# A fixed order for a program's beginning: transfers by need, the first group's norms on VectorE, its queries batch by batch

## The chip, the core and the metric

The kernel runs on one core of a Trainium2 chip. The metric is the device time of one launch in microseconds (us). Four executions of the kernel before took 1539.61 to 1543.85 us, with a median of 1542.02 us.

The names of the engines are those of the profile: PE (TensorE, matrix products; PEld is its loading of weights), DVE (VectorE), ACT (ScalarE), POOL (GpSimd) and SP (SyncE, which here issues nearly all transfers, in the order of its queue). Each engine runs its own instructions strictly in order and waits, by semaphores, for results of the others.

## The reference

Two transformer layers over x (64 batches of 128 rows of 128 numbers). Layer 0 attends from the normed x to 128 rows of a side input and 120 rows of a context, with 16 heads of 8, and then sends each row to two of eight experts. Layer 1 attends to the context alone and has small experts of its own. Everything is float32. Cut to its frame:

```python
x = x + _L0_xattn_ref(_layernorm(x), fside_BxSxS_0, ctx_1024, ctx_1024, ...)
x = x + _L0_ffn_ref(_layernorm(x), L0_ffn_wqkv, L0_ffn_w1, L0_ffn_w2)
x = x + _L1_xattn_ref(_layernorm(x), ctx_1024, ctx_1024, ...)
x = x + _L1_ffn_ref(_layernorm(x), L1_ffn_Wg, L1_ffn_bg, L1_ffn_W1, L1_ffn_W2)

def _L0_xattn_ref(x1, x2, memory_k, memory_v, Wq, bq, Wk, bk, Wv, bv, Wp, bp):
    q = heads(x1 @ Wq + bq)
    k = heads(concatenate([x2 @ Wk + bk, memory_k], axis=1))
    v = heads(concatenate([x2 @ Wv + bv, memory_v], axis=1))
    attn = softmax(einsum('bhqd,bhkd->bhqk', q, k) * scale)
    return merge(einsum('bhqk,bhkd->bhqd', attn, v)) @ Wp + bp
```

## The kernel before

The 64 batches stand in 16 groups of 4 (`GB`), and x stays in SBUF, one tile of [128, 4, 128] per group (`xg`). The attention of layer 0 is one loop over iterations `it`, a software pipeline: iteration `it` computes the row maxima of batch `it` (`max_bank`: products L344 on PE, reductions L356 on DVE), adds them as a shift to the queries of the batch before (`shift`: transposes L401, DVE L404), computes the shifted scores of batch `it - 2` and their exponentials (`score_bank`: L372 on PE, L380 on ACT), multiplies the exponentials of batch `it - 3` with the values (`values`: L417), and finishes batches `it - 3` and `it - 4` (`out1` to `out5`). The rounds of an iteration come in two halves, `rounds(0, 1)` and `rounds(2, 3)`, of four banks for the maxima and four for the scores each. All products go through eight PSUM banks that are handed out in turn (`mtile`).

Queries, keys and values of a group are made in the iterations ahead of it (`prep`): in a regular group, keys (`prep_k`: L187 on PE, L192 on ACT) and values (`prep_v`: L199 on PE, L206 on DVE) when `it` is 2 modulo 4, the transposed normed rows (`prep_x`: L165 on PE, L166 on ACT) when it is 3, and the queries (`prep_q`: L269 on PE, four activations L273 on ACT, one for each of four slots) when it is 0, two activations in each half.

The norms of layer 0 are split: DVE takes statistics of each batch (`Norm.stats`, L113), and POOL puts them together for a group of four in nine small operations (`put_together`, L127 to L135, of which the last is a power), makes the normed rows (`normed`, L156) and then adds the output bias to x (L465).

The beginning lies outside the hand-ordered part of the program (`tc.manual_schedule`, within which the engines keep the order in which the code names their instructions); there the scheduler places instructions by its own priorities. SP's queue begins with four groups of x, the three masks, eight tensors of layer 0's weights and biases, a block of zeros for the experts' rows, the router's weights and three constants, and then kvT of group 0 (the side input, transposed), the context's keys and values (`context`, L247 and L250), and kvT of group 1; twelve more groups of x and layer 1's weights follow. Before the loop, all of group 0 is prepared, for four batches at a time: keys, values, transposes, queries. Group 1's transposes and queries (`norm_of(1)`, `prep_x(1)` and `prep_q(1, ·)`) are placed in iterations 0 and 1.

Layer 1 begins in another way: `prep_batch(j)` (L284 to L301) makes the queries of one batch of group 0, with one transpose (L293), one copy (L294), one product (L296) and four activations of 128 columns (L298), batch 0 ahead of the loop and the others in the first three iterations. In layer 0 this function isn't used before the change.

The lines of the kernel that the text speaks of are these; an instruction's line in the profile is the line here.

Of the kernel before, what the change touches and what calls it, by code (L numbers as in the profile page):

```python
# [8 lines left out]
F32 = mybir.dt.float32  # L9
# [9 lines left out]
GB = 4  # L19
NG = B // GB  # L20
S = 128
# [23 lines left out]
def transformer_kernel(ctx, tc, a, out):  # L45
# [29 lines left out]
    def load_row(name, n):  # L75
        return load_const(name, [128, n], a[name].partition_broadcast(128))

    def attention_weights(p):
        return dict(
            wq=load_const(p + "wq", [D, D], a[p + "wq"]),  # L80
            wk=load_const(p + "wk", [D, D], a[p + "wk"]),
            wv=load_const(p + "wv", [D, D], a[p + "wv"]),
            wo=load_const(p + "wo", [D, D], a[p + "wo"]),
            bq=load_const(p + "bq", [128, NS], a[p + "bq"]),
            bk=load_const(p + "bk", [128, NV], a[p + "bk"]),
            bv=load_row(p + "bv", D),
            bo=load_row(p + "bo", D),
        )

    hmask = load_const("hmask", [128, NS], a["hmask"])  # L90
    kmask = load_const("kmask", [128, NV], a["kmask"])
    smask = load_const("smask", [128, NV], a["smask"])
    l0 = attention_weights("a0_")


    stat = ctx.enter_context(tc.tile_pool(name="stat", bufs=4))
# [2 lines left out]
    class Norm:  # L99
# [18 lines left out]

        def put_together(self, g):

# [26 lines left out]
                self.mv[:, b0:b1, 0], self.mv[:, b0:b1, 0], -1.0, 1.0, ALU.mult, ALU.mult  # L147
            )

        def normed(self, g, pool=rows, bufs=1, width=D, xn=None, js=range(GB)):  # L150

            if xn is None:
                xn = pool.tile([S, GB, width], F32, name="xn", tag="xn", bufs=bufs)
            for j in js:
                b = g * GB + j
                nc.gpsimd.tensor_scalar(  # L156
                    xn[:, j, :D], xg[g][:, j, :], self.mv[:, b, 0:1], self.rstd[:, b : b + 1],
                    ALU.add, ALU.mult,
                )
            return xn  # L160
# [13 lines left out]
    for s in range(2):  # L174
        k = keep.tile([128, NV, GB, KF + KC], F32, name=f"k2_{s}", tag=f"k2_{s}")
        K2.append(k)
        v = keep.tile([KF, GB, H // 2, 2, 32], F32, name=f"v_{s}", tag=f"v_{s}")
        nc.gpsimd.memset(v, 0.0)
        for i in range(2):
            nc.gpsimd.memset(v[:, :, :, i, 16 * i + HD : 16 * i + HD + 1], 1.0)  # L180
        VS.append([v])
        m = keep.tile([S, 2, 128], F32, name=f"nm_{s}", tag=f"nm_{s}")
        nc.gpsimd.memset(m, 0.0)
        NM.append(m)

    def keys_of(w, src, g, n0, pk):
        nc.tensor.matmul(  # L187
# [29 lines left out]
    def attention(layer, w, norm, first, aside):  # L217
# [5 lines left out]
        with ExitStack() as es:  # L223
# [13 lines left out]
            def loads(g):  # L237
# [2 lines left out]
                nc.sync.dma_start(t, a["fsideT" if first else "ctxT"][:, g * GB : (g + 1) * GB, :])  # L240
                src[g] = t

            def context(g):
                if first:
                    s = g % 2
                    for v in range(NV):
                        nc.sync.dma_start(  # L247
                            k2[s][:, v, :, KF:], a["ctx_k"][:, v, g * GB : (g + 1) * GB, :]
                        )
                    nc.sync.dma_start(  # L250
                        vs[s][1].rearrange("k b h i w -> k b (h i w)"),
                        a["ctx_v"][:, g * GB : (g + 1) * GB, :],
                    )

            def mtile():
                return banks.tile([128, 512], F32, name="bank", tag="bank")
# [204 lines left out]
            def norm_of(g):  # L461
                if g < NG:
                    normed[g] = norm.normed(g)

                    nc.gpsimd.tensor_tensor(  # L465
                        xg[g], xg[g], w["bo"].unsqueeze(1).to_broadcast([S, GB, D]), ALU.add
                    )

            if first:
                loads(0)  # L470
                context(0)
                yield
                norm_of(0)
                prep_k(0)
                prep_v(0)
                prep_x(0)
                prep_q(0, 0)
                prep_q(0, 1)
            else:
                prep_batch(0)  # L480
            loads(1)
            oTs, pos_ = {}, {}

            for it in range(B + (4 if first else 5)):
# [24 lines left out]
                if first:  # L509

                    on(3, out2)
                    prep(it, 0)
                    rounds(2, 3)
                    on(1, shift)
                    on(3, out3)
                    aside.call(it, mtile)
                    on(4, out4, out5)
                    aside.ahead(it)
                    prep(it, 1)
                    aside.call(it, mtile)  # L520
                    aside.end(it, work, mtile)
                else:
                    if it < GB - 1:
                        prep_batch(it + 1)
                    prep(it, 0)
                    on(4, out3)
                    on(3, out2)
                    on(5, out4)
                    prep(it, 1)
                    on(1, shift)  # L530
                    on(5, out5)
                    aside.ahead(it)
                    if it == GB - 1 or it > GB and it % GB == 1:
                        norm_of(it // GB + 1)
                    if it == 1:

                        nc.gpsimd.tensor_tensor(
                            xg[0], xg[0], w["bo"].unsqueeze(1).to_broadcast([S, GB, D]), ALU.add
                        )
# [171 lines left out]
    def logits1(rt, lg, n, l):  # L711
# [16 lines left out]
    nc.vector.memset(zero, 0.0)  # L728
    filled = []


    spare = nc.sync.dma_start(
        xs[E * CAP - TT :].rearrange("(h p) d -> p h d", p=S),
        zero,
    )
    AFTER = mybir.DependencyInfo(mybir.DependencyClass.Sync, mybir.DependencyReason.DATA)
    DEEP = 4
    scatters = []

    def behind(ins, earlier):  # L740
        for e in earlier:
# [2 lines left out]
    def scatter(probe, j, k, xn):  # L744
# [11 lines left out]
        behind(s, [scatters[-DEEP] if len(scatters) >= DEEP else spare])  # L756
        tc.add_to_no_dep_group("scatters", s.ins)
        scatters.append(s)

# [314 lines left out]
    class Aside0(Ahead):  # L1074
# [8 lines left out]
        def lead(self, b):  # L1083
            norms[0].stats(b)
            if b % GB == GB - 1:
                norms[0].roots(b + 1 - GB, b + 1)

        def made(self, b):
            norms[1].stats(b)

# [12 lines left out]
            for _ in self.tiles:  # L1103
                pass

    wr0 = load_const("wqkvT", [D, 3 * E], a["wqkvT"])
# [3 lines left out]
    rp = ctx.enter_context(tc.tile_pool(name="route", bufs=1))  # L1110
    aside0 = Aside0()
    steps = attention(0, l0, norms[0], True, aside0)
    next(steps)
    for b in range(GB):
        aside0.lead(b)
    next(steps)
    for g in range(4, NG):
        load_x(g)
    l1 = attention_weights("a1_")
# [248 lines left out]
```

## Time and profile before

| | us |
|---|---|
| median of 4 runs (lowest, highest) | 1542.02 (1539.61, 1543.85) |
| the profiled execution | 1541.85 |
| its span, first to last instruction | 1540.1 |
| PE busy in the span | 1423.1 (92%) |
| DVE busy | 1057.0 (69%) |
| ACT busy | 838.4 (54%) |
| POOL busy | 641.6 (42%) |

A row of a timeline has the start, the length, the engine, the line, the operation, what it writes and reads, the shapes, and a count if several stand together; in brackets is the idle time of the engine ahead of it and what ended it. PE's float32 products appear as two passes each, so a group of 16 products is a row of x32. The chain of waits is followed back from the last instruction; each of its rows is what the end depended on at that moment.

SP's own rows show how the beginning's transfers are issued (start, time taken by the issue):

```profile
0.74 2.09 SPq L58 DMA_DIRECT2D x<-in_x  x4
...
11.07 0.43 SPq L240 DMA_DIRECT2D kvT<-in_fsideT  x1
11.55 0.98 SPq L247 DMA_DIRECT2D k<-in_ctx_k  x2
12.57 0.56 SPq L250 DMA_DIRECT2D vc<-in_ctx_v  x1
13.18 0.36 SPq L240 DMA_DIRECT2D kvT<-in_fsideT  x1
13.59 16.26 SPq L58 DMA_DIRECT2D x<-in_x  x12
```

### The profile page before, as it was taken

How to read it: one execution, taken by the hardware profiler on the slowest of the kernel's cores; microseconds unless marked ns; L12 is line 12 of the kernel's file. 1: busy time of each engine (PE TensorE's matmuls, PEld its weight loads, DVE VectorE, ACT ScalarE, POOL GpSimd, SP SyncE). 2: the span in 40 equal slices, each digit the busy share in tenths (PEclk: the TensorE clock that was granted, in tenths of full speed). 3: DMA queues.
4: the chain of work that ended last, by engine and by line, in shares of the span. 5: the costliest groups of instructions: out<-in, count | busy, mean ns of one | idle time of the engine just before them, and what ended most of it. 6: DMA issues, size and time to landing. Idle time of an engine off the chain costs nothing.

```text
span 1540.1 us, 44916 instructions
## 1 busy us (share of the span) xinstructions
PE 1423.1 (92%) x18156; PEld 1149.2 (75%) x18156; DVE 1057.0 (69%) x2923; ACT 838.4 (54%) x1722; POOL 641.6 (42%) x1211
## 2 busy tenths in 40 slices
PE   5999999999999999989999995799899999999997
PEld 3777777777777777878888885577677777777775
DVE  4777888888888987454544442467776767778764
ACT  2766666667666656433333331366665666666653
POOL 4223255656564635542000002677645555543200
PEclk9999999999999999999999998589999999999999
DMA  8421122222222221567766664111101111110000
GB/s 191 113 53 49 47 58 64 64 62 61 62 64 60 59 72 47 171 181 218 206 201 184 195 194 116 28 36 34 30 29 36 29 30 42 33 31 16 16 9 28
DMA packets 124130, 123.91 MB, mean 80 GB/s; under 512 B 47122, under 2 KB 106514, under 8 KB 122002
## 3 DMA queue, kind: packets, MB, share of 16 engines
q1 hardware_dynamic: 115730, 103.71, 24.7%
q0 software_dynamic: 8192, 17.32, 3.6%
q8 instruction: 144, 2.36, 0.6%
q14 instruction: 64, 0.52, 0.1%
HBM read 97.31 MB, written 23.67 MB: 79 GB/s over the span
## 4 chain that ended last, share of the span: by engine, by line
PE 77%; DVE 8%; DMA 5%; POOL 4%; ACT 4%; issue 2%; SPq 0%; POOLq 0%; ACTq 0%; DVEq 0%
PE bank L372 15%; PE bank L344 12%; PE bank L417 11%; PE bank L997 9%; PE bank L1246 4%; PE bank L1225 4%; DVE nm L356 4%; PE bank L1010 3%; DMA q<-xs 2%; PE bank L433 2%; PE bank L401 2%; PE bank L269 2%; PE bank L187 2%; PE bank L615 2%; PE bank L199 2%
## 5 line engine op out<-in xcount | busy, mean ns | idle before, releaser
L356 DVE TENSOR_REDUCE nm<-bank 128x2 f32<-128x496 f32 (+1 forms) x768 | 462.4, 663 | 193.2 <-PE bank L344 118.5
L372 PE MATMUL bank<-q,k 32*120 32x256 f32 (+1 forms) x3072 | 467.4, 406 | 7.4 <-DVE q L404 2.4
L380 ACT ACTIVATE p<-bank 120x512 f32<-120x512 f32 (+1 forms) x768 | 402.5, 601 | 108.5 <-PE bank L372 57.6
L344 PE MATMUL bank<-k,q 32*128 32x248 f32 (+1 forms) x4096 | 452.6, 344 | 2.3 <-ACT q L273 1.3
L344 PEld LDWEIGHTS bank<-k,q 32*128 32x128 f32 x4096 | 350.5, 190 | 61.6 <-issue 25.3
L372 PEld LDWEIGHTS bank<-q,k 32*120 32x120 f32 (+1 forms) x3072 | 298.8, 181 | 38.1 <-DVE nm L356 17.1
L1002 DVE TENSOR_TENSOR p<-p,bank 128x256 f32<-128x256 f32 x213 | 88.4, 420 | 132.1 <-ACT p L1001 132.1
L417 PE MATMUL bank<-p,v 128*32 128x128 f32 (+1 forms) x4096 | 177.3, 278 | 0.0
L751 POOL DMA_INDIRECT xs<-xn,at x128 | 128.7, 1006 | 52.8 <-issue 29.5
L426 ACT COPY ov<-bank 128x256 f32<-128x256 f32 x128 | 47.4, 370 | 180.1 <-PE bank L417 180.1
L1157 POOL DMA_INDIRECT yb<-ys,back x128 | 123.7, 967 | 32.2 <-issue 24.7
L1001 ACT ACTIVATE p<-bank 128x256 f32<-128x256 f32 x213 | 81.0, 383 | 100.8 <-PE bank L997 99.3
L417 PEld LDWEIGHTS bank<-p,v 128*32 128x32 f32 (+1 forms) x4096 | 110.2, 110 | 25.9 <-issue 8.2
L997 PE MATMUL bank<-q 128*128 128x256 f32 x516 | 118.7, 380 | 1.8 <-ACT q L988 1.8
L404 DVE SCALAR_TENSOR_TENSOR q<-bank,c_smask,q 128x256 f32<-128x256 f32 x256 | 111.3, 477 | 7.8 <-PE bank L401 5.2
L156 POOL TENSOR_SCALAR xn<-x,mv,rstd 128x128 f32<-128x128 f32 x256 | 111.2, 447 | 11.7 <-PE bank L165 5.8
L417 PE MATMUL bank<-p,vc 120*32 120x128 f32 x2048 | 104.4, 273 | 0.4 <-issue 0.4
L997 PEld LDWEIGHTS bank<-q 128*128 128x128 f32 x516 | 94.7, 190 | 13.2 <-ACT q L988 2.1
L1143 POOL MEMSET gates<- 128x256 f32 x2 | 0.6, 312 | 246.4 <-DMA ys<-q 246.4
L273 ACT ACTIVATE q<-bank,c_a_bq,c_hmask 128x512 f32<-128x512 f32 x124 | 89.7, 780 | 16.2 <-PE bank L269 16.2
L144 POOL TENSOR_SCALAR rstd<-mv 128x4 f32<-128x4 f32 (+1 forms) x33 | 6.5, 197 | 216.5 <-DVE mv L117 132.3
L997 PE MATMUL bank<-vc 128*128 128x256 f32 x336 | 78.9, 385 | 0.0
(201 smaller groups left out, 2259.1 us busy)
## 6 DMA issues: line engine op xcount, KB each, us to landing
q<-in_w SPq DMA_DIRECT2D x43, 576.0 KB, 4.9
vc<-in_w SPq DMA_DIRECT2D x28, 576.0 KB
vc<-in_ctx_v SPq DMA_DIRECT2D x16, 960.0 KB, 6.9
k<-in_ctx_k SPq DMA_DIRECT2D x32, 240.0 KB
q<-xs SPq DMA_DIRECT2D x43, 128.0 KB, 2.1
ys<-q SPq DMA_DIRECT2D x43, 128.0 KB, 2.2
x<-in_x SPq DMA_DIRECT2D x16, 256.0 KB, 5.4
kvT<-in_fsideT SPq DMA_DIRECT2D x16, 256.0 KB, 12.3
```

The costliest lines, as they stand in the source:

```text
L156: nc.gpsimd.tensor_scalar(xn[:, j, :D], xg[g][:, j, :], self.mv[:, b, 0:1], self.rstd[:, b : b + 1], ALU.add, ALU.mult,)
L273: nc.scalar.activation(q4s[g][:, :, s, :], pq.rearrange("p (b q) -> p b q", b=GB), AF.Identity, bias=w["bq"][:, s : s + 1], scale=hmask[:, ...
L344: nc.tensor.matmul(pa[:, u, :], lhsT=q4s[g][r, j, s, :], rhs=k2[g % 2][r, s // 2, j, :], start=True, stop=True,)
L356: nc.vector.tensor_reduce(nm[b % 2].rearrange("q i (a s) -> q a i s", s=16)[:, 2 * ra + v : 2 * ra + v + len(slots) // 2, :, 0], pa.rearra ...
L372: nc.tensor.matmul(pb[:n, v * 256 : (v + 1) * 256], lhsT=k2[g % 2][r, v, j, k0 : k0 + n], rhs=q4s[g][r, j, 2 * v : 2 * v + 2, :].rearrange ...
L380: nc.scalar.activation(ps_[b][:n, c, ra, :], pb[:n], AF.Exp, scale=SCALE)
L404: nc.vector.scalar_tensor_tensor(q, pm, smask[:, v : v + 1], q, ALU.mult, ALU.add)
L417: nc.tensor.matmul(pav[32 * ra : 32 * ra + 32, v * S : (v + 1) * S], lhsT=vs[g % 2][c][:, j, 4 * v + ra, i, :], rhs=p[:n, c, ra, (2 * v + ...
L751: s = nc.gpsimd.indirect_dma_start(xs, bass.IndirectOffsetOnAxis(at[:, j, k : k + 1], 0), xn, None)
L997: nc.tensor.matmul(ph[:, u, :], lhsT=w[:, c, u * 128 : (u + 1) * 128], rhs=xT, start=True, stop=True)
L1002: nc.vector.tensor_tensor(hT[:, c, :], sa, ph[:, 1, :], ALU.mult)
L1157: nc.gpsimd.indirect_dma_start(y[:, k, b % 2, :], None, ys, bass.IndirectOffsetOnAxis(back[:, b, k : k + 1], 0),)
```

## The change

The beginning goes under a manual schedule too, with SP among the ordered engines. Four things follow.

The transfers stand in a new order: x of group 0, wk, bk, kmask, kvT of group 0; wq, bq, hmask, the context's keys; wv, bv, smask, x of group 1, the context's values, kvT of group 1; wo, bo, x of groups 2 and 3, the router's constants and the block of zeros; then, as before, twelve groups of x and layer 1's weights.

Group 0's norms are made by `Norm.alone`: statistics, their aggregation, the addition of epsilon and the normed rows on DVE, and only the power on POOL; first for batch 0 alone, then for batches 1 to 3.

Ahead of the loop stand only the keys of group 0 and `prep_batch(0)`. Batches 1 to 3 are prepared between the two halves of iterations 0 to 2, group 0's values at the end of iteration 0. Group 1's transposes move from iteration 0 to iteration 2, and its four query activations from iteration 1 to the middle of iteration 3. The bias is added to x of group 0 in iteration 1 (`biased(0)`).

The zeroing of the second `v` tile on POOL goes behind the powers, the zeroing of `nm` goes from POOL to DVE, and the normed rows have two buffers instead of one.

```diff
-    for g in range(4):
-        load_x(g)
+    begin = ctx.enter_context(ExitStack())
+    begin.enter_context(tc.manual_schedule(engines=ORDERED | {ET.SP}))
+    load_x(0)
...
+    l0 = attention_weights("a0_", ("wk", "bk"))
     kmask = load_const("kmask", [128, NV], a["kmask"])
...
+        def alone(self, b0, b1, xn):
+            for b in range(b0, b1):
+                st = stat.tile([S, 6], F32, name="st", tag="st")
+                nc.vector.bn_stats(st, xg[b // GB][:, b % GB, :])
+                nc.vector.bn_aggr(self.mv[:, b, :], st)
+            r = self.rstd[:, b0:b1]
+            nc.vector.tensor_scalar(r, self.mv[:, b0:b1, 1], EPS, None, ALU.add)
+            nc.gpsimd.tensor_tensor(r, r, power.to_broadcast([S, b1 - b0]), ALU.pow)
+            for b in range(b0, b1):
+                nc.vector.tensor_scalar(
+                    xn[:, b % GB, :], xg[b // GB][:, b % GB, :], self.mv[:, b, 0:1],
+                    self.rstd[:, b : b + 1], ALU.subtract, ALU.mult,
+                )
...
-        def normed(self, g, pool=rows, bufs=1, width=D, xn=None, js=range(GB)):
+        def normed(self, g, pool=rows, bufs=2, width=D, xn=None, js=range(GB)):
...
+                if half == 0 and it < GB - 1:
+                    prep_batch(it + 1)
                 if (it, half) == (0, 1):
+                    prep_v(0)
                     norm_of(1)
+                if (it, half) == (1, 1):
+                    biased(0)
+                if (it, half) == (2, 1):
                     prep_x(1)
+                if (it, half) == (3, 0):
+                    prep_q(1, 0)
+                    prep_q(1, 1)
...
-                elif j == 0 and it or it == 1:
+                elif j == 0 and it:
                     prep_q(g, half)
...
             if first:
                 loads(0)
-                context(0)
                 yield
-                norm_of(0)
+                context_k(0)
+                yield
+                context_v(0)
+                loads(1)
+                yield
                 prep_k(0)
-                prep_v(0)
-                prep_x(0)
-                prep_q(0, 0)
-                prep_q(0, 1)
+                prep_batch(0)
+                yield
             else:
                 prep_batch(0)
-            loads(1)
+                loads(1)
...
+        def begin(self):
+            self.xn = rows.tile([S, GB, D], F32, name="xn", tag="xn", bufs=2)
+            norms[0].alone(0, 1, self.xn)
+            norms[0].alone(1, GB, self.xn)
...
+    next(steps)
+    l0.update(attention_weights("a0_", ("wq", "bq")))
+    hmask = load_const("hmask", [128, NS], a["hmask"])
+    next(steps)
+    l0.update(attention_weights("a0_", ("wv", "bv")))
+    smask = load_const("smask", [128, NV], a["smask"])
+    load_x(1)
+    next(steps)
+    l0.update(attention_weights("a0_", ("wo", "bo")))
+    for g in range(2, 4):
+        load_x(g)
+    nc.sync.dma_start(wr0, a["wqkvT"])
...
+    aside0.begin()
+    zeros_and_ones(VS[1][0])
+    next(steps)
+    begin.close()
     for g in range(4, NG):
         load_x(g)
```

More of the change, by code (lines that the diff above doesn't have):

```diff
@@ L76, in load_row, with attention_weights @@
         return load_const(name, [128, n], a[name].partition_broadcast(128))
[L78 to L90, printed above, removed]
+    def attention_weights(p, names=("wq", "wk", "wv", "wo", "bq", "bk", "bv", "bo")):
+        columns = {"bq": NS, "bk": NV}
+        return {
+            n: load_row(p + n, D) if n in ("bv", "bo")
+            else load_const(p + n, [D, columns.get(n, D)], a[p + n])
+            for n in names
+        }
+    l0 = attention_weights("a0_", ("wk", "bk"))
     kmask = load_const("kmask", [128, NV], a["kmask"])
-    smask = load_const("smask", [128, NV], a["smask"])
-    l0 = attention_weights("a0_")
     stat = ctx.enter_context(tc.tile_pool(name="stat", bufs=4))
@@ L177, in transformer_kernel, with zeros_and_ones @@
         v = keep.tile([KF, GB, H // 2, 2, 32], F32, name=f"v_{s}", tag=f"v_{s}")
+        VS.append([v])
+        m = keep.tile([S, 2, 128], F32, name=f"nm_{s}", tag=f"nm_{s}")
+        nc.vector.memset(m, 0.0)
+        NM.append(m)
+    def zeros_and_ones(v):
         nc.gpsimd.memset(v, 0.0)
@@ L180, in transformer_kernel @@
             nc.gpsimd.memset(v[:, :, :, i, 16 * i + HD : 16 * i + HD + 1], 1.0)
[L181 to L184, printed above, removed]
+    zeros_and_ones(VS[0][0])
     def keys_of(w, src, g, n0, pk):
@@ L241, in loads, with context_k, context_v @@
                 src[g] = t
+            def context_k(g):
+                for v in range(NV):
+                    nc.sync.dma_start(
+                        k2[g % 2][:, v, :, KF:], a["ctx_k"][:, v, g * GB : (g + 1) * GB, :]
+                    )
+            def context_v(g):
+                nc.sync.dma_start(
+                    vs[g % 2][1].rearrange("k b h i w -> k b (h i w)"),
+                    a["ctx_v"][:, g * GB : (g + 1) * GB, :],
+                )
             def context(g):
                 if first:
[L245 to L253, printed above, removed]
+                    context_k(g)
+                    context_v(g)
             def mtile():
@@ L463, in norm_of, with biased @@
                     normed[g] = norm.normed(g)
-                    nc.gpsimd.tensor_tensor(
-                        xg[g], xg[g], w["bo"].unsqueeze(1).to_broadcast([S, GB, D]), ALU.add
-                    )
+                    biased(g)
+            def biased(g):
+                nc.gpsimd.tensor_tensor(
+                    xg[g], xg[g], w["bo"].unsqueeze(1).to_broadcast([S, GB, D]), ALU.add
+                )
             if first:
                 loads(0)
-                context(0)
                 yield
-                norm_of(0)
+                context_k(0)
[3 more added lines that the diff above has]
+                yield
                 prep_k(0)
-                prep_v(0)
-                prep_x(0)
-                prep_q(0, 0)
-                prep_q(0, 1)
+                prep_batch(0)
+                yield
             else:
                 prep_batch(0)
-            loads(1)
+                loads(1)
             oTs, pos_ = {}, {}
@@ L535, in attention @@
                     if it == 1:
-                        nc.gpsimd.tensor_tensor(
-                            xg[0], xg[0], w["bo"].unsqueeze(1).to_broadcast([S, GB, D]), ALU.add
-                        )
+                        biased(0)
                     if it == GB - 1:
@@ L729, in transformer_kernel @@
     filled = []
[L732 to L735, printed above, removed]
     AFTER = mybir.DependencyInfo(mybir.DependencyClass.Sync, mybir.DependencyReason.DATA)
     DEEP = 4
-    scatters = []
+    scatters, spare = [], []
     def behind(ins, earlier):
@@ L755, in scatter @@
             tc.declare_no_dep(s.ins, group="scatters", reason="rows of their own")
-        behind(s, [scatters[-DEEP] if len(scatters) >= DEEP else spare])
+        behind(s, [scatters[-DEEP] if len(scatters) >= DEEP else spare[0]])
         tc.add_to_no_dep_group("scatters", s.ins)
@@ L1086, in lead, with normed @@
                 norms[0].roots(b + 1 - GB, b + 1)
+        def begin(self):
+            self.xn = rows.tile([S, GB, D], F32, name="xn", tag="xn", bufs=2)
+            norms[0].alone(0, 1, self.xn)
+            norms[0].alone(1, GB, self.xn)
+        def normed(self, j):
+            return self.xn
         def made(self, b):
@@ L1104, in rest @@
                 pass
-    wr0 = load_const("wqkvT", [D, 3 * E], a["wqkvT"])
+    rp = ctx.enter_context(tc.tile_pool(name="route", bufs=1))
+    wr0 = const.tile([D, 3 * E], F32, name="c_wqkvT", tag="c_wqkvT")
+    aside0 = Aside0()
+    steps = attention(0, l0, norms[0], True, aside0)
+    next(steps)
[10 more added lines that the diff above has]
+    nc.sync.dma_start(wr0, a["wqkvT"])
     upper = load_const("upper", [128, 128], a["upper"])
@@ L1109, in transformer_kernel @@
     first_row = load_row("first_row", E)
-    rp = ctx.enter_context(tc.tile_pool(name="route", bufs=1))
-    aside0 = Aside0()
-    steps = attention(0, l0, norms[0], True, aside0)
+    spare.append(
+        nc.sync.dma_start(xs[E * CAP - TT :].rearrange("(h p) d -> p h d", p=S), zero)
+    )
+    aside0.begin()
+    zeros_and_ones(VS[1][0])
     next(steps)
-    for b in range(GB):
-        aside0.lead(b)
-    next(steps)
+    begin.close()
     for g in range(4, NG):
```

## The prediction

> **What bounds the kernel now.** I read the 40 slices of the span first (busy tenths, 38.5 us each), since the change is about the program's beginning:
>
> ```profile
> PE   5999999999999999989999995799899999999997
> ```
>
> PE is at nine tenths nearly everywhere; the first slice (5) is the lowest. There I read the chain of waits over the first 80 us (start us, length us, what):
>
> ```profile
> 11.07 3.28 DMA kvT<-in_fsideT
> 14.49 2.04 PE bank L187 x2
> 16.53 1.71 PE bank L199 x8
> 18.24 0.87 PE bank L165 x4
> 19.13 0.59 ACT xnT L166
> 19.77 2.09 PE bank L269 x2
> 21.88 0.79 ACT q L273
> 22.70 2.07 PE bank L344 x12
> 24.83 4.04 DVE nm L356 x7
> ```
>
> The first matmul waits until 14.49 for kvT, the 21st transfer in SP's queue; iteration 0 begins at 22.70. Then the timeline by engine (start us, length, engine, line, operation):
>
> ```profile
> 16.57 1.44 ACT L192 ACTIVATE k<-bank,c_a_bk,c_kmask 128x512 f32<-128x512 f32 x2 [6.16 <-PE bank L187]
> 24.83 9.39 DVE L356 TENSOR_REDUCE nm<-bank 128x2 f32<-128x496 f32 x16 [5.74 <-PE bank L344]
> 34.67 0.79 PE L372 MATMUL bank<-q,k 32*128 32x256 f32 x1 [2.38 <-DVE q L404]
> 42.94 0.42 PE L417 MATMUL bank<-p,v 128*32 128x128 f32 x8
> ```
>
> Iterations 0 and 1 are paced by DVE (sixteen reductions without a gap). Iteration 2 begins for PE at 34.67, when the first shifted queries (L404, begun at 34.14) are there. Call that moment S; batch 0's values (L417) follow at 43.0, S + 8.3, and batch 1's at 51.04, 8.0 later. From there the program is in its regular rhythm, which the change leaves alone, so what counts is how much earlier that third mark comes.
>
> Last, busy time by stretch (us, then PE busy, count, granted clock, DMA share, GB/s): the first half of iteration 2 beside that of iteration 3.
>
> ```profile
> 34.67:37.97 3.30, 3.30 (x31) 0.56 0.37 50
> 44.84:46.75 1.91, 1.91 (x36) 1.00 0.95 188
> ```
>
> PE stood still from 32.3 to 34.67, and the same work then took 3.30 us instead of 1.91, at a granted clock of 0.56.
>
> **The change, part by part, up to S.** In the new order SP issues x_0, wk, bk, kmask, kvT. SP's rows cost 0.52 us for an x and 0.48 for a constant, so kvT is issued at 0.74 + 0.52 + 3 x 0.48 = 2.70 instead of 11.07. From issue to use it took 3.42 us before, x_0 2.73: usable at 5.4 to 6.1; I take its own row, 6.1. The two tiles of ctx_k go out at about 4.6 and 5.1 (their lanes are free by then: each transfer from the ninth on waits for the one eight places before it). Landing is bounded by x_0's 2.7 us below and the median of the four times larger ctx_v, 6.9 us, above: 7.8 to 12.0, against a need at 11.3; so 0 to 0.7 us, taken as 0, as each carries a quarter of ctx_v's bytes.
>
> The norms: statistics 0.29, aggregation 0.18 and three more short steps on DVE and one power on POOL (0.71 for two columns at L145) put batch 0's rows at about 5.2 (x_0 at 3.47, steps of some 1.7 in all); keys are not done before 8.1, so this costs nothing; without that cover it would be late only if x_0 were 3 us late. POOL's second zeroing of v (1.81 us) goes behind the powers and is needed only at the second prep_v.
>
> Keys: 6.1 + 2.04 = 8.14; ACT evacuates them until 8.18 + 1.44 = 9.62 and only then copies batch 0's transposed rows. For that chain the kernel has an example, layer 1's own batch-wise start:
>
> ```profile
> 965.81 0.27 ACT L294 COPY xnT<-bank 128x128 f32<-128x128 f32 x1 [20.84 <-PE bank L293]
> 966.13 0.79 PE L296 MATMUL bank<-xnT,c_a_wq 128*128 128x128 f32 x2 [0.35 <-ACT xnT L294]
> 966.96 1.50 ACT L298 ACTIVATE q<-bank,c_a_bq,c_hmask 128x128 f32<-128x128 f32 x4 [0.89 <-PE bank L296]
> 967.47 3.57 PE L344 MATMUL bank<-k,q 32*128 32x120 f32 x32 [0.55 <-ACT q L298]
> ```
>
> Copy to first query 1.15, to first L344 1.66: first L344 at 9.62 + 1.66 = 11.3, where it was 22.70. Second query slot done at 9.62 + 1.15 + 0.35 + 0.46 = 11.58; before, its end (23.33) was 1.50 ahead of the first reduction, so DVE begins at 13.1.
>
> DVE then has, up to S: 16 reductions 9.39, and in between what was done early before: four statistics of group 1 (half of 1.86: 0.93) and the two v additions (0.76); then 0.53 from the first shift to PE. S = 13.1 + 9.39 + 0.93 + 0.76 + 0.53 = 24.7; before 34.67. **Gained: 10.0 us.** The transposes and query products of batches 1 and 2 and the eight value products that move into iterations 0 and 1 are PE and ACT work beside DVE: 2 x (0.47 + 0.35 + 0.79) + 1.9 = 5.1 us of PE in 11 us. Should PE be late with a bank, DVE waits; bound 0 to 1.2 us (reductions 5 to 8 of iteration 0 come out of PE at 16.3 rather than 15.5 and the same again in iteration 1 if it runs at half clock); I take 0, since 10 to 12 L344 passes started per half microsecond there.
>
> **Iteration 2.** Batch 3's preparation now stands in it. PE reaches its transpose at S + 3.3, but ACT's copy queues behind four exponentials (done before at 39.20, S + 4.5): copy until S + 4.8, product until S + 5.35, keys of group 1 (1.12) until S + 6.45, where before they were done by S + 4.4. ACT: four query activations to S + 6.9, keys 1.45 to S + 8.35, and only then the second half's exponentials. The last score bank of round 3 reuses the bank that the keys hold, as it did before (idle until the release by L192 at 40.63): PE resumes at S + 8.4, ends the rounds at S + 9.2, then shift 0.4, group 1's transposes 0.5 (formerly in iteration 0), values of v 0.9: L417 at S + 11.0 instead of S + 8.3. **Lost: 2.7 us.**
>
> **Iteration 3.** Group 1's four query activations (2.78) now stand between the two sets of exponentials; before they ran beside the reductions, for nothing. From L417 on: first exponentials end 5.07 later as before, queries at 7.9, the bank they release stops PE until then (about 1.5 us), rounds end at 8.75, exponentials at 10.05, the next L417 at 10.1 against 8.0: 2.1. The nearest whole row is iteration 8, which prepares a group's queries too: L417 from 85.87 to 96.49, 10.62, which makes it 2.6. I take 2.3. **Lost: 2.3 us.**
>
> **The clock.** In both versions PE idles ahead of S, so the 3.30 of the first half is in both sums. After it the changed kernel has two waits (0.9 and 1.0 us) that the old one had not. If the clock returns as it did at 37.5, nothing is lost; if it stays at half to the end of iteration 2, keys cost 1.81 instead of 1.12 and the last rounds and values end later: 1.3 us. In layer 1's stop-and-go start it stayed at 0.50 from 962 to 989. Between 0 and 1.3 I take 0.6.
>
> [...]
>
> Everything else: the second xn buffer removes waits of POOL on L165, 5.8 us in all, off the chain: nothing. The later transfers keep their order; group 1's ctx_k is issued at 38.3 to 39.3 before and needed by PE at 53.8. Now it is needed at about 49, still 10 us later: nothing.
>
> Sum: 10.0 - 2.7 - 2.3 - 0.6 = 4.4. The profiled execution took 1541.85 (1540.1 of span, 1.75 around it), 0.2 below the median. 1541.85 - 4.4 = **1537.5**.
>
> **Rivals.** (a) *The head start is kept*: iterations 2 and 3 lose 1 us each, because exponentials and activations interleave better than my queue has it. For: ACT is busy only some 8 of 10 us there. Against: the bank that L192 releases stopped PE already before. 10.0 - 2.0 = 8.0: 1533.8. Chance 0.14.
> (b) *Half clock through iteration 3*: 1.3 in iteration 2, and in iteration 3 values 1.9 (32 passes took 1.93 at 1002.85, 64 took 1.90 at 60.52), first rounds 1.4, queries 1.0 (2.08 against 1.12), the rest 1.1 behind ACT's wait: 5.4. 5.0 - 1.3 - 5.4 = -1.7, 1543.6, and from 1539 up where it ends on the way: within the noise. For: two new waits in iteration 2 and one of 1.5 us in iteration 3; against: the return at 37.5. Chance 0.2.
> (c) *The slower side*: the same half clock as in layer 1, 24 us from S on. Place: iterations 2 to 4. It adds iteration 4's values and rounds, 1.9 + 1.4, to (b): 1541.85 + 1.7 + 3.3 = 1546.9. For: layer 1's rows. Against: at 34.67 it took PE 2.9 us to come back, with the same two kinds of matmul. It decides against the change from about S + 19 on. Chance 0.1.
> (d) *The early transfers don't come in time*, so that the new order gives little: ctx_k lands late and iteration 0 waits. For: a share of 1.1 and 290 GB/s were the most that the engines moved at 25 us, and five transfers stand ahead; against: these are 0.65 MB, some 2.3 us at that rate. Each microsecond beyond 11.3 costs one: with ctx_k at 15, 1541.2. Chance 0.06.
> My forecast, 1535 to 1540: 0.5.
>
> **How the numbers follow.** This kernel's runs spread by 0.27%; 0.2% is about what can be told from no change: 1538.9 to 1545.1. Faster: (a) and nearly all of the forecast, 0.63. Same: (b), most of (d) and the forecast's rim, 0.25. Slower: (c) and tails, 0.12. The range, 1533.0 to 1542.0, takes in (a) and most of (b), and leaves out (c).
>
> **What would show it.** First L344 near 11.3 and first reduction near 13; PE's first L372 near 24.7; first L417 11 us after that and the second 10 us on, near 46; idle time of PE in iterations 2 and 3 ended by ACT's keys and queries. I am wrong in the first part if kvT or ctx_k lands late, in the second if L417 comes S + 8.3 as before, in the third if PE's clock stays at 0.5 beyond the middle of iteration 3.

## The result, and the profile after

The changed kernel took 1539.46 us, the median of 42 runs (1534.38 to 1543.94), where the kernel before took 1542.39 (63 runs, 1538.15 to 1547.33): a ratio of 0.998, with a 95% interval of 0.9975 to 0.9986, or 2.2 to 3.9 us. The profiled execution of the changed kernel is one of its fastest: 1535.65 us, with a span of 1533.9; for the kernel before it was 1541.85 and 1540.1.

In the slices of the span, the first has risen from five tenths to seven:

```profile
PE   7999999999999999989999995699999999999997
```

The lines of the code have moved: maxima L344 are now L373, reductions L356 are L385, scores L372 are L401, exponentials L380 are L409, values L417 are L446, shifted queries L404 are L433; keys are L202 (ACT: L207), group-wise transposes L176, group-wise queries L289 and L293, and the batch-wise steps L313 to L318. In the experiments below a few lines more or fewer stand ahead of them. The timeline after, with the columns of the one before:

```profile
10.72 2.39 PE L373 MATMUL bank<-k,q 32*128 32x248 f32 x16 [0.55 <-ACT q L318]
...
12.78 2.42 DVE L385 TENSOR_REDUCE nm<-bank 128x2 f32<-128x496 f32 x4 [3.01 <-PE bank L373]
...
16.66 2.42 DVE L385 TENSOR_REDUCE nm<-bank 128x2 f32<-128x496 f32 x4 [1.46 <-PE bank L373]
...
25.60 0.79 PE L401 MATMUL bank<-q,k 32*128 32x256 f32 x1 [1.80 <-DVE q L433]
...
37.50 0.43 PE L446 MATMUL bank<-p,v 128*32 128x128 f32 x8
...
45.48 0.47 PE L401 MATMUL bank<-q,k 32*120 32x256 f32 x1 [1.25 <-ACT q L293]
...
47.45 0.43 PE L446 MATMUL bank<-p,v 128*32 128x128 f32 x8
```

The first maxima begin 12.0 us earlier than before (22.70), the first reductions too (24.83). DVE then waits 1.46 us for PE in iteration 0, which it did not do before, and it has 1.60 us of work among its reductions that it did ahead of the loop before (statistics 0.86, v additions 0.74, as forecast). So S, PE's first scores of iteration 2, comes at 25.60: 9.07 us ahead of 34.67. Batch 0's values are only 5.44 us ahead (37.50 against 42.94), and batch 1's only 3.52 (47.45 against 50.97). In iteration 3 PE waits 1.25 us for ACT's queries of group 1, a wait that the profile before does not have.

SP's rows, for the two transfers that the start waits for and for the next group's:

```profile
2.72 0.43 SPq L255 DMA_DIRECT2D kvT<-in_fsideT  x1
...
4.62 0.98 SPq L260 DMA_DIRECT2D k<-in_ctx_k  x2
...
35.45 1.05 SPq L260 DMA_DIRECT2D k<-in_ctx_k  x2
```

kvT was usable at 5.64. No instruction of the first iterations needs to wait for one of the later transfers; the one row that names such a transfer is taken up below.

Busy time by stretch (us, then PE, PEld, DVE, ACT, POOL, each with its count, PE's granted clock, DMA share, GB/s), from just before S to the middle of iteration 2:

```profile
24.20:25.60 1.40, 0.00 (x0) 0.00 (x0) 1.40 (x4) 0.00 (x0) 1.32 (x2) 0.50 1.22 300
25.60:29.30 3.70, 3.70 (x31) 2.86 (x31) 2.47 (x7) 1.08 (x2) 2.47 (x10) 0.50 1.08 278
29.30:31.30 2.00, 1.04 (x7) 0.75 (x5) 1.26 (x2) 1.24 (x3) 2.00 (x4) 0.50 0.68 170
31.30:34.40 3.10, 3.10 (x15) 1.46 (x18) 0.00 (x0) 2.67 (x6) 2.47 (x4) 0.50 0.28 52
```

The clock is at half from 24.2 to 34.4, 10.2 us; in the profile before it was at half for 3.4 us only, from 34.1. Between 29.30 and 31.30 PE is busy for half the time: it waits for ACT's copy of batch 3's rows:

```profile
30.38 0.27 ACT L314 COPY xnT<-bank 128x128 f32<-128x128 f32 x1
...
30.70 0.80 PE L316 MATMUL bank<-xnT,c_a_wq 128*128 128x128 f32 x2 [0.96 <-DMA c_a_wv<-in_a_wv]
```

The second row puts the wait down to a transfer of layer 1's weights, which this product does not read. It begins 0.05 us after the copy ends, and the same wait in again and again2 (below) is put down to the copy, so the copy is taken to be what ended it. From S to the first mark below, batch 0's values, 3.6 us of the early start are lost.

### The profile page after: what moved, and what is told of

Its sections match the earlier page's. It is cut to its first block, busy times and chain, and to the rows that moved or that the text cites. A ratio compares the mean times of both kernels' runs of the same rounds, so it can differ in the third digit from the quotient of the medians.

```text
span 1533.9 us, 44940 instructions
## 1 busy us (share of the span) xinstructions
PE 1419.3 (93%) x18162; PEld 1145.7 (75%) x18162; DVE 1061.3 (69%) x2935; ACT 842.5 (55%) x1737; POOL 641.1 (42%) x1198
## 4 chain that ended last, share of the span: by engine, by line
PE 74%; DVE 7%; POOL 5%; DMA 5%; ACT 4%; issue 2%; SPq 2%; POOLq 0%; DVEq 0%; ACTq 0%
PE bank L401 14%; PE bank L446 11%; PE bank L373 11%; PE bank L1022 9%; PE bank L1297 4%; PE bank L1276 4%; PE bank L1035 3%; DVE nm L385 3%; DMA q<-xs 2%; PE bank L462 2%; PE bank L430 2%; PE bank L645 2%; PE bank L289 2%; DMA vc<-xs 2%; POOL xs L776 2%
## 5 line engine op out<-in xcount | busy, mean ns | idle before, releaser
L385 DVE TENSOR_REDUCE nm<-bank 128x2 f32<-128x496 f32 (+1 forms) x768 | 462.6, 663 | 193.9 <-PE bank L373 115.4
L401 PE MATMUL bank<-q,k 32*120 32x256 f32 (+1 forms) x3072 | 466.4, 405 | 7.0 <-DVE nm L385 2.2
L409 ACT ACTIVATE p<-bank 120x512 f32<-120x512 f32 (+1 forms) x768 | 402.6, 601 | 109.4 <-PE bank L401 62.1
L373 PE MATMUL bank<-k,q 32*128 32x248 f32 (+1 forms) x4096 | 453.7, 344 | 2.4 <-ACT q L318 1.6
L373 PEld LDWEIGHTS bank<-k,q 32*128 32x128 f32 x4096 | 349.9, 190 | 62.2 <-issue 26.6
L401 PEld LDWEIGHTS bank<-q,k 32*120 32x120 f32 (+1 forms) x3072 | 298.3, 181 | 37.0 <-DVE nm L385 16.5
L446 PE MATMUL bank<-p,v 128*32 128x128 f32 (+1 forms) x4096 | 176.4, 278 | 0.0
L446 PEld LDWEIGHTS bank<-p,v 128*32 128x32 f32 (+1 forms) x4096 | 109.5, 110 | 25.8 <-issue 8.2
L433 DVE SCALAR_TENSOR_TENSOR q<-bank,c_smask,q 128x256 f32<-128x256 f32 x256 | 111.3, 477 | 7.8 <-PE bank L430 5.2
L446 PE MATMUL bank<-p,vc 120*32 120x128 f32 x2048 | 103.2, 272 | 0.0
L293 ACT ACTIVATE q<-bank,c_a_bq,c_hmask 128x512 f32<-128x512 f32 x120 | 87.0, 782 | 11.2 <-PE bank L289 11.1
```

What stands on the lines that cost most here:

```text
L293: nc.scalar.activation(q4s[g][:, :, s, :], pq.rearrange("p (b q) -> p b q", b=GB), AF.Identity, bias=w["bq"][:, s : s + 1], scale=hmask[:, ...
L373: nc.tensor.matmul(pa[:, u, :], lhsT=q4s[g][r, j, s, :], rhs=k2[g % 2][r, s // 2, j, :], start=True, stop=True,)
L385: nc.vector.tensor_reduce(nm[b % 2].rearrange("q i (a s) -> q a i s", s=16)[:, 2 * ra + v : 2 * ra + v + len(slots) // 2, :, 0], pa.rearra ...
L401: nc.tensor.matmul(pb[:n, v * 256 : (v + 1) * 256], lhsT=k2[g % 2][r, v, j, k0 : k0 + n], rhs=q4s[g][r, j, 2 * v : 2 * v + 2, :].rearrange ...
L409: nc.scalar.activation(ps_[b][:n, c, ra, :], pb[:n], AF.Exp, scale=SCALE)
L433: nc.vector.scalar_tensor_tensor(q, pm, smask[:, v : v + 1], q, ALU.mult, ALU.add)
```

## The experiments

The experiments ran on three chips, B, C and D; chip A is that of the profiles above, and the record doesn't say whether it is one of the three. On chip B the kernel before took 1615.52 us (median of 27 runs), on C and D 1542.7 (11 runs) and 1542.9 (17 runs). Times are therefore compared by their ratio to the kernel before on the same chip. Up to S the beginning agrees to 0.3 us between the chips (34.67 and 34.96 before, 25.60 to 25.85 after), so it is read from three marks in each trace: the first values (L446) of batches 0, 1 and 2, which the expectations call the first, second and third mark. (The third mark of the prediction, batch 1's values, is the second of these.) All results in one table:

| kernel (chip) | S | first, second, third mark | half clock in the first 60 us: start (length) | ratio to before, 95% interval |
|---|---|---|---|---|
| before (A) | 34.67 | 42.94, 50.97, 60.45 | 34.1 (3.4) | |
| before2 (D) | 34.96 | 44.55, 52.57, 61.23 | 33.8 (6.8) | one execution, profiled |
| after (A) | 25.60 | 37.50, 47.45, 56.11 | 24.2 (10.2) | 0.998, 0.9975 to 0.9986 |
| again (B) | 25.77 | 37.66, 47.62, 56.28 | 24.6 (10.2) | one execution, profiled |
| again2 (D) | 25.85 | 37.03, 47.53, 57.23 | 25.9 (3.4), 46.3 (3.4) | 0.9985, 0.9973 to 0.9996 |
| transfers_only (B) | 34.08 | 42.60, 50.63, 59.29 | 34.4 (3.4) | 0.9989, 0.9974 to 1.0005 |
| batch3_early (B) | 25.78 | 34.74, 45.47, 54.95 | 26.7 (3.4), 43.8 (3.4) | 0.9955, 0.9935 to 0.9976 |
| fill_pe (B) | 25.90 | 35.48, 45.42, 54.08 | none | 0.9949, 0.9927 to 0.9971 |
| split_q1 (C) | 25.87 | 36.96, 45.83, 54.49 | 26.7 (6.8) | one execution, profiled |
| norms_pool (C) | 25.84 | 36.92, 47.11, 57.13 | 26.1 (3.4), 46.6 (3.4) | one execution, profiled |
| group_wise (C) | 27.45 | 36.40, 46.35, 55.01 | 27.4 (3.4) | one execution, profiled |
| group_fill (D) | 27.19 | 34.54, 44.49, 53.15 | none | one execution, profiled |
| group_fill_split (D) | 27.41 | 34.77, 43.65, 52.31 | none | one execution, profiled |
| best3 (C) | 25.99 | 33.36, 42.23, 50.89 | none | 0.9949, 0.9936 to 0.9962 |

**The changed kernel again (again, again2).** No edit.

> The changed kernel once more, for a second profile. In the first one the change was ahead of the kernel before by 4.34 us from iteration 5 of layer 0 on, the half-clock stretch of the beginning lasted from 24.2 to 34.4, and the medians over all runs differ by only 2.9 us. Theory A (the steps on record: the order of the engines' queues sets the marks, the clock adds about 1 us): the marks are the same within 0.5 us up to PE's first L401 (25.6), and iteration 5 is ahead by 4.3 +- 1. [...]

> The changed kernel without an edit, for a third trace of its beginning. Theory A (the time in the beginning is set by the program, and the length of the half-clock stretch by it): half clock for 10.2 us from 24 to 25 on, first values 37.4 to 37.8, third mark 56.0 to 56.4. [...]

The first repeats the marks of the profile after within 0.17 us, and it has 10.2 us of half clock too, from 24.6 instead of 24.2. The second has S 0.25 us later, but half clock for only 3.4 us in iteration 2, and then a second stretch of 3.4 us from 46.3, against theory A. So the program alone does not set how much half clock the beginning has. All stretches in the table are 3.4, 6.8 or 10.2 us long, and where they start differs from execution to execution by 0.4 to 1.7 us with the same S to within 0.25. No program was traced twice on one chip, so a share of the chip in this is not excluded. The first mark was 0.5 us earlier and the third 1.1 us later than in the profile after.

**The kernel before again (before2).** No edit.

> The kernel before once more, for a second trace of its first iterations. In its first trace PE stood for 0.7 us in the values of the third mark's iteration without anything to wait for that the profile shows, and that iteration took 9.48 us, where nearly every changed version took 8.66. Theory A (a chance stall of one execution): the distance from the second to the third mark is 8.6 to 8.8 us, and the changed kernel's real gain at the third mark is 3.5 us instead of 4.3. Rival B (it belongs to the kernel before): 9.4 to 9.6 us again. First mark at 42.8 to 43.2, second 8.0 to 8.1 later.

The distance from the second to the third mark was 8.66 us: theory A. The 9.48 in the first trace holds a chance wait: in its values PE stood 0.4 us, and its weight loads 0.7 us, for nothing that the profile shows ("issue"). That trace thus gave the changed kernel 0.8 us too much at the third mark. In return this execution had 6.8 us of half clock, and its first mark came 9.59 us after S, not 8.27.

**The new order of transfers without the rest (transfers_only).** Group 0's norms on POOL and its queries for four batches at once ahead of the loop, group 1's norms, transposes and queries in iterations 0 and 1, as they were.

```diff
-                if half == 0 and it < GB - 1:
-                    prep_batch(it + 1)
                 if (it, half) == (0, 1):
-                    prep_v(0)
                     norm_of(1)
+                    prep_x(1)
...
+                norm_of(0)
                 prep_k(0)
-                prep_batch(0)
+                prep_v(0)
+                prep_x(0)
+                prep_q(0, 0)
+                prep_q(0, 1)
...
-    aside0.begin()
+    for b in range(2 * GB):
+        aside0.lead(b)
```

> The new order of transfers and the fixed order of the beginning alone; group 0 is prepared as before the change, four batches at a time, its norms on POOL and its values ahead of the loop, and group 1's queries in iterations 0 and 1 beside the reductions. Theory A (the head start comes from the transfers, and the queries made in iterations 2 and 3 give most of the further gain back): first maxima at about 15 instead of 10.7, S at about 27 instead of 25.6, but L417 of batch 0 at S + 8.3 and iteration 5 ahead of the kernel before by 7 to 8 us, more than the whole change's 4.3; time about 1534.5. Rival B (the batch-wise queries carry the gain): ahead by less than 4, time 1539 or more.

The third mark gained 1.2 us against the first trace of the kernel before, and the ratio can't be told from no change, so the expectation failed. The timeline shows where:

```profile
15.06 4.36 PE L364 MATMUL bank<-k,q 32*128 32x248 f32 x32 [0.87 <-ACT q L293]
...
17.23 1.27 POOL L488 TENSOR_TENSOR x<-x,c_a_bo 128x512 f32<-128x512 f32 x1 [8.04 <-DMA c_a_bo<-in_a_bo]
...
21.14 1.80 POOL L195 MEMSET v<- 128x2048 f32 x1
...
23.44 1.89 PE L176 MATMUL bank<-ident,xn 128*128 128x128 f32 x4 [4.02 <-POOL xn L167]
...
27.32 2.42 DVE L376 TENSOR_REDUCE nm<-bank 128x2 f32<-128x496 f32 x4 [5.46 <-PE bank L364]
```

The first maxima did come 7.6 us earlier (15.06). But group 1's transposes stood in iteration 0, and their normed rows came late: POOL waited 8.04 us for the output bias, which the new order issues only at 9.09 and which took 8.1 us to land, added it to x, put group 1's norms together, and zeroed the second `v`, all ahead of them. PE waited 4.02 us, DVE 5.46 and, in the next iteration, 1.48. An earlier start moves the work forward and leaves POOL's queue where it was. In the change group 1's transposes stand in iteration 2 and the bias of group 0 behind group 1's norms, and nothing in iterations 0 and 1 waits for POOL; which of the two moves does it was not tried.

**Norms on POOL (norms_pool).** Only group 0's norms go back.

```diff
-            norms[0].alone(0, 1, self.xn)
-            norms[0].alone(1, GB, self.xn)
+            for b in range(GB):
+                self.lead(b)
+            norms[0].normed(0, xn=self.xn)
```

> Group 0's norms go the old way: statistics on DVE, put together and normed on POOL for the four batches at once, ahead of POOL's second zeroing of v. Theory A (the prediction's: the norms are under the cover of the keys, so VectorE's norms bring nothing by themselves): first normed rows of batch 0 at about 7.9, while ACT copies its transposed rows only at 9.1; first maxima (L373) within 0.3 us of 10.72 and first values within 0.4 us of 37.5 to 37.7. Rival B (VectorE's norms are what lets the first batch start early): first maxima at 11.5 or later and the first values later by 0.8 or more.

The first maxima began at 10.97, and in again2, which had the same half-clock stretches, at 10.98; the marks differ by 0.11, 0.42 and 0.10 us. POOL's normed rows begin at 7.44, and ACT copies the first transposed rows only at 9.31, behind the keys:

```profile
7.44 1.74 POOL L167 TENSOR_SCALAR xn<-x,mv,rstd 128x128 f32<-128x128 f32 x4
...
9.31 0.26 ACT L314 COPY xnT<-bank 128x128 f32<-128x128 f32 x1
```

Theory A: the norms on DVE bring nothing by themselves. (The first mark, 36.92, is earlier than either theory had it; the run had less half clock in iteration 2 than the profile after.)

**Queries for four batches at once (group_wise, group_fill).** The rest of the change stays; group_fill adds the sixteen transposes of fill_pe (below).

```diff
-                if half == 0 and it < GB - 1:
-                    prep_batch(it + 1)
...
+                normed[0] = aside.normed(0)
                 prep_k(0)
-                prep_batch(0)
+                prep_x(0)
+                prep_q(0, 0)
+                prep_q(0, 1)
```

> Everything of the change stays except the batch-wise queries: group 0's transposes and queries are made for four batches at once ahead of the loop, after the keys; values of group 0 stay at the end of iteration 0, group 1's parts where the change put them. Theory A (batch 3's preparation inside iteration 2 takes back what the earlier start gives): first maxima later, at 13.5 to 14.2 instead of 10.72, first scores of iteration 2 at 26.9 to 27.6 instead of 25.6, but values only 9.7 to 10.4 after them instead of 11.9, so at 37.0 to 37.8: no difference to the changed kernel of more than 0.5 us. Rival B (batch by batch is where the gain is): first values at 39 or later.

> The group-wise queries of the earlier experiment, and the sixteen unread transposes at the end of iteration 1, so that the clock no longer differs between the two ways. Theory A (apart from the clock the batch-wise queries with batch 3 in iteration 2 are worth nothing): no half clock in the first 60 us or one window of 3.4 us at most, third mark at 53.8 to 54.6, within 0.5 us of the batch-wise version with the same transposes (54.08). Rival B (group-wise is better apart from the clock as well): 53.5 or earlier. Rival C (batch-wise is better once the clock is held): 54.7 or later.

```profile
14.13 4.36 PE L371 MATMUL bank<-k,q 32*128 32x248 f32 x32 [0.87 <-ACT q L293]
...
27.45 0.79 PE L399 MATMUL bank<-q,k 32*128 32x256 f32 x1 [2.89 <-DVE q L431]
```

Against split_q1 on the same chip (11.00 and 25.87), the first maxima are 3.1 us later and S 1.6, since DVE no longer waits for PE within iteration 0. The first mark then comes 8.95 us after S, and at 36.40 is earlier than the changed kernel's and than theory A of group_wise had it (9.7 to 10.4 after S, 37.0 to 37.8), with half clock for 3.4 us. group_fill and fill_pe both have the clock at full speed throughout, one trace each on two chips: the first mark comes 7.35 us after S in group_fill and 9.58 in fill_pe, so batch 3's preparation inside iteration 2 costs 2.2 us (best3, which makes it an iteration earlier, has 7.37), where the batch-wise start had gained 1.3 at S. The third mark is 0.93 us earlier group by group: rival B of group_fill. Batch by batch, as the change has it, loses about 1 us.

**PE kept busy (fill_pe).** Sixteen transposes of the identity, read by nobody, at the end of iteration 1.

```diff
                 if (it, half) == (1, 1):
+                    fill = mtile()
+                    for _ in range(16):
+                        nc.tensor.transpose(fill[:, :S], ident, ident)
                     biased(0)
```

> The changed kernel with sixteen transposes of the identity more at the end of iteration 1, whose results nothing reads; they fill PE's wait for the first shifted queries (23.8 to 25.6). Theory C (the clock): the array is back at full clock by 28 instead of 34.4, iteration 2 shortens by 1 to 2 us, iteration 5 ahead by 5.3 to 6.3. Theory A alone (ACT's queue sets the end of iteration 2): the clock returns sooner, but L417 of batch 0 moves by less than 0.7 us; if the transposes run over the wait, S comes up to 1 us later.

The same stretches as above:

```profile
24.20:25.90 1.70, 1.55 (x12) 1.03 (x10) 1.70 (x4) 0.00 (x0) 1.62 (x3) 1.00 1.07 295
25.90:29.30 3.40, 2.23 (x31) 1.72 (x31) 3.34 (x9) 2.23 (x5) 2.15 (x10) 1.00 1.10 294
```

The idle time ahead of S is filled, the clock stays full, and the same 31 matmuls take 2.23 us instead of 3.70: theory C. The third mark is 2.2 us earlier than in again on the same chip. Work that computes nothing made the beginning shorter. The transposes also take a bank and so move every later tile on by one, which could have changed a wait; but PE's waits from 24 to 62 us are those of again2 (1.2 us for ACT's queries, 1.2 and 1.1 for the copy, 0.6 for the keys), apart from the one ahead of S. The four traces with the transposes (fill_pe, best3, group_fill, group_fill_split) have no half clock in the first 60 us, and each of the ten without them has some.

**Batch 3 prepared earlier (batch3_early).**

```diff
-                if half == 0 and it < GB - 1:
+                if half == 0 and it < GB - 2:
                     prep_batch(it + 1)
...
                 if (it, half) == (1, 1):
+                    prep_batch(3)
                     biased(0)
```

> The changed kernel, with batch 3's queries made at the end of iteration 1, where PE and ACT wait for DVE, instead of the middle of iteration 2. Theory A (ACT's queue in iteration 2, four query activations and the keys ahead of the exponentials, costs 2 us or more): S unchanged within 0.5, L417 of batch 0 at S + 9.5 instead of S + 12.0, iteration 5 ahead by 6.3 to 7; time about 1537. Rival C (the clock at half speed is what makes iteration 2 long): L417 still at S + 11 or later, no more than 1 us gained.

The first mark came 8.96 us after S instead of 11.89 (again), which holds both this edit and 6.8 us less of half clock; a stretch from 43.8 then cost some of it, and 1.3 us were left at the third mark, less than expected. Alone it can't separate the two.

**Group 1's queries in two halves (split_q1).**

```diff
                 if (it, half) == (3, 0):
                     prep_q(1, 0)
+                if (it, half) == (3, 1):
                     prep_q(1, 1)
```

> Half of group 1's query activations (two of four, L293) moves from the middle of iteration 3 to its end. Theory A (my prediction's step: iteration 3 is longer because all four activations, 2.79 us on ACT, stand between its two sets of exponentials and hold a bank): the wait of PE on ACT's q (1.25 us) goes, the distance between the first and the second mark of the values' start falls from 9.95 to between 8.4 and 9.2 us, and the third mark comes at 54.9 to 55.6 instead of 56.1 to 56.3. First mark unchanged, 37.5 to 37.7. Rival B (it is the heavier stretch as a whole, PE and ACT together, that takes the time): the distance stays at 9.7 or more, or the third mark stays at 56.0 or more because the next iteration pays.

```profile
42.11 1.45 ACT L293 ACTIVATE q<-bank,c_a_bq,c_hmask 128x512 f32<-128x512 f32 x2
43.45 2.29 ACT L410 ACTIVATE p<-bank 120x512 f32<-120x512 f32 x4
...
45.77 1.47 ACT L293 ACTIVATE q<-bank,c_a_bq,c_hmask 128x512 f32<-128x512 f32 x2
```

The second pair now follows the exponentials. PE's wait of 1.25 us is gone and the distance from the first to the second mark is 8.87 us instead of 9.95; the next distance is unchanged at 8.66. Theory A for the distance; the first mark was to stay at 37.5 to 37.7 and came at 36.96, with 6.8 us of half clock instead of 10.2, so that the third mark, 54.49, holds both.

**Three edits together (best3), and their group-wise counterpart (group_fill_split).** batch3_early, fill_pe and split_q1 in one kernel; and group_fill with split_q1.

> Three edits together on the changed kernel: batch 3 prepared at the end of iteration 1, sixteen unread transposes behind it so that TensorE does not stand still, and group 1's queries in two halves. Theory A (the three losses of my sum, in iteration 2, iteration 3 and by the clock, are separate and add): no stretch of half clock in the first 60 us, first values at 33.2 to 34.2, second 8.6 to 9.6 later, third mark at 51.3 to 53.0, 7.5 to 9 us ahead of the kernel before; ratio 0.9935 to 0.9955. Rival B (they are one loss counted three times: ACT is the limit of these iterations): third mark at 53.5 or later, ratio 0.995 to 0.997, no better than one of the edits alone.

> The group-wise queries, the sixteen transposes, and group 1's queries in two halves: the counterpart of the three edits together, which had its third mark at 50.89. Theory A (batch by batch is worth something once batch 3 is not in iteration 2): third mark at 52.2 to 53.0, 1.3 to 2.1 us behind. Rival B (no way of preparing group 0 is better than the other): 51.5 or earlier.

The third mark of best3 came at 50.89, better than expected, 5.2 us ahead of the profile after; its distances are 7.37, 8.87 and 8.66. The ratio to the kernel before is 0.9949, 0.9936 to 0.9962: 7.9 us, and its interval lies wholly below the changed kernel's. It can't be told from that of fill_pe, also 0.9949, so that three edits are worth more than one rests on the marks. The group-wise counterpart is 1.42 us later at the third mark (theory A): batch by batch does gain something, once batch 3 is not prepared in iteration 2.

## Why the prediction was right, step by step

The forecast was 1537.5 us, 4.4 less than the profiled execution's 1541.85; the median came to 1539.46, 2.9 less than that of the kernel before.

**The start: 10.0 predicted, 9.1 measured.** First maxima at 10.72 instead of 11.3, first reductions at 12.78 instead of 13.1. The mis-sized term is PE's delay of a bank in iteration 0: bounded at 0 to 1.2 us and taken as 0, it was 1.46. That the early transfers would land in time was right, which disposes of rival (d). That the norms cost nothing was right, and they bring nothing either.

**Iteration 2: 2.7, and 0.6 for the clock, predicted; 3.6 measured.** The sum had the first values at S + 11.0, with 1.4 us of half clock already in its first half (3.30 instead of 1.91), so at S + 9.6 at full clock. fill_pe, at full clock, has 9.58, and it shows the wait that the sum was built on, PE held until ACT's keys release a bank, at S + 6.8, where the sum has S + 8.4 with the 1.4 us in it, 7.0 without:

```profile
32.73 0.47 PE L404 MATMUL bank<-q,k 32*120 32x256 f32 x1 [0.58 <-ACT k L207]
```

The clock cost 2.3 us in the profile after (11.90) and 1.6 in again2 (11.18), where the sum had 1.4 + 0.6 = 2.0. The program alone does not set which of these a trace shows: the changed kernel without an edit had half clock for 10.2 us at the beginning (after, again) and for 3.4 us (again2). The 0.6 was an estimate between 0 and 1.3, and the two traces lie on both sides of the sum that it makes.

**Iteration 3: 2.3 predicted, 1.9 measured.** The distance was 9.95 instead of 8.03. split_q1 shows that 1.1 of it is the second pair of activations ahead of the exponentials.

**From there the regular rhythm.** True, but against a chance wait in the trace before: 9.07 - 3.63 - 1.92 makes 3.52 at the second mark, and that wait made it 4.34 at the third, beside a prediction of 4.4. That agreement is luck: the steps themselves sum to 0.9 less than forecast. before2 and again2 give 4.0; the mean third marks of two traces before (60.84) and three after (56.54) differ by 4.3.

**Of that, 2.9 us reach the median, and the rest is open.** Up to iteration 60 the lead holds: means of 590.5 and 586.4 us for that batch's values in the two traces before and the two after on chips A and D, 4.1. At the end of the span it is 3.6 (1539.9 and 1536.3), and the medians say 2.2 to 3.9. Between lie the experts' products, where PE waits for gathered rows 15.8 and 15.2 us before, 19.0 and 15.8 after, and layer 1's start, at half clock for 37.5 and 34.1 us before, 30.7 and 41.0 after. Two traces each don't settle which of them takes the last microsecond.

**The rivals.** (a), the head start kept, did not happen in the change; best3 reaches about the 8.0 us of (a) (7.9 by its ratio) with three edits that each take out one loss. (b), half clock in iteration 3, did happen by chance in again2 and norms_pool, for 3.4 us: again2's second distance is 0.55 us and its third 1.04 us longer than in the profile after, 1.6 together, where (b) had 5.4 us behind iteration 2 for half clock throughout. (c) needed 24 us of it from S on; the longest was 10.2. In (d) the prediction counts five transfers ahead of the context's keys, where SP's rows show eight, whose size is the 0.65 MB that it gives.

What the prediction lacked is the netting of the batch-wise queries: their gain sat in the 10.0 and their cost in the 2.7, and set against each other they lose 0.9 us.

## What to carry to other kernels

When a pipeline's start is brought forward, cost each moved step where it lands: here iterations 2 and 3 took back 5.5 of 9.1 us, and three small edits (batch 3's part one iteration up, half of group 1's queries half an iteration down, the idle gap filled) returned 5.2 at the third mark. Ask of each engine that was not sped up (here POOL's queue) whether its results still come in time. And where PE stands idle just ahead of a dense stretch (here for 1.80 us ahead of S), price a half clock there (31 matmuls took 3.70 us in the profile after and 2.23 in fill_pe), or fill the gap with matmuls that nobody reads (here sixteen, with the third mark 2.2 us earlier).

## What the runs showed of the hardware

In the 3.4 us ahead of the clock's fall to half PE's records were busy for 3.02 us (profile after), 1.59 (before) and 1.60 (again2). It came back after 3.4 us in which PE was busy for 2.83 us or more (before, again2, batch3_early), and stayed at half where it was busy for 2.00 to 2.52 (after, split_q1). As it fell after 3.02 us and came back after 2.83, the busy time of these records alone does not settle what the clock does next. At the start of the program the granted clock is recorded as 1.00 while the key pair took 2.04 us (at 14.49 before, at 5.64 after), where it takes 1.02 at 29.63 in fill_pe.

One chip ran the same program 5% slower (B: 1615.52 us for the kernel before, against 1542.7 on C and 1542.9 on D). Its beginning is the same to 0.2 us, but iterations 24 to 40 took 154.7 us instead of 147.3, at a granted clock of 1.00 throughout a stretch of 143 us in both. In its waits of PE (us in total, times, longest) one row is large that the profile after does not have:

```profile
PE bank L446 <- issue: 12.8, 36, 1.0
```

The values waited there for nothing that the profile shows; these 12.8 us are a sixth of the 78 us by which the two spans differ, and it is the same kind of wait as the single one in the trace before. What it is was not tried.
